# A graph attention layer before a mixture of experts: the opening rewritten up to the branch

## The chip, the cores and the metric

The program runs on one core of one Trainium2 chip. A core has TensorE (PE in the profile, its weight loads PEld), VectorE (DVE), ScalarE (ACT), GpSimd (POOL) and SyncE (SP), which issues transfers only. The metric is the device time of one execution in microseconds.

## The reference, cut to what matters

Everything is float32, with 4096 tokens of 256 numbers. The first part is a graph attention layer with four heads of 64, the second a mixture of 8 experts of which each token uses two. Only the first part is touched.

```python
xn  = layernorm(x)
h   = einsum('nd,hdk->hnk', xn, W)
s_col, s_row = (h * a1).sum(-1), (h * a2).sum(-1)
e   = leaky_relu(s_row[:, :, None] + s_col[:, None, :], 0.2)
att = softmax(where(adj > 0, e, NEG_INF), axis=-1)      # adj: 4096 x 4096
out = concat_over_heads(att @ h)
y   = elu(out) + xn @ Wr + br
x   = x + gamma * layernorm(y) + beta
x   = x + moe(layernorm(x))
```

## The kernel before, in words

The tokens are taken in 8 blocks of 512 (`B`), a block in four tiles of 128 (`TB`); two blocks make a range of 1024 rows (`R`, `HB` = 2), so there are four ranges. A softmax weight of a column token j and a row token i is made without an exponential of its own: up to a factor of the row that cancels, it is the larger of a row factor `er` and a column factor `eb`, masked by the adjacency; another column factor `ed` is multiplied into the projected values `ha`. VectorE does that in one instruction for a head and a tile j (`weigh`, L1353, `w<-er,eb,am`). TensorE multiplies `w` with `ha` into `acc` (L835) and with `unit` into `den` (L844), which sums the weights. `w` has ten buffers. This form holds only where the scores keep within a limit. A flag is computed from the weights; a branch goes to a general arm (not run with these inputs) or to the arm described here.

The row factors must stand along the free dimension and be the same on all 128 partitions, while the projection leaves them with a token on each partition. So `store_parts` transposes them to 16 rows, copies them (L792) and stores them to memory, and `load_rows` (L800) reads them back as a broadcast over all partitions.

**The opening, before the branch.** Small vectors and weights are loaded on ACT's queue, `x` by SP. 37 warm-up matmuls run (`WARM`). `norm_block(0)` computes mean and variance of block 0 (`bn_stats`, L176 and L177), one over the root by integer halving and three Newton steps (L159 to L168), scales the rows on ACT (L623), transposes them on TensorE (L630) and copies them out (L643). `scores_weights` multiplies W by a1 and a2, which gives eight more columns of the projection, and finds limit and flag. `project_first` projects block 0 into four accumulators (L747) and makes its factors, `factor_first` the scaled `ha`, `residual_first` xn @ Wr (L778). Then block 1 is normalised and transposed. Masks of the first tiles are made on ACT from adjacency slabs of 128x1024 (L1236).

**Behind the branch.** For the first four tiles j only the first half of range 0 is attended (block 0 is known), then the same tiles' second half, then full tiles. TensorE's order is written out by hand (`queue`, `order_of`, with `strict`): it follows the order of the program. `prepare_at(s)` stands between the tiles' matmuls and puts the preparation of the next block there, a piece for each step s: s = 0 to 3 follow the first halves, s = 4 to 7 the second halves, larger s the full tiles. `norm_steps` (statistics; ACT scaling; transposes) takes three steps and `project_steps` four. VectorE's and ACT's orders are made by the scheduler from priorities and dependencies; `tc.issue_after` holds a group of instructions behind a given one. Both arms are followed by the experts' stage, from some 785 us on.

## Time and profile before

| what | us |
|---|---|
| median of 3 runs (lowest, highest) | 1281.69 (1279.56, 1282.52) |
| the profiled execution | 1287.53 |
| its span, first to last instruction | 1285.8 |
| TensorE busy | 1255.5 |
| VectorE busy | 847.7 |
| the opening, to ACT's last work before the branch | 25.03 |
| TensorE's first attention matmul | 30.84 |
| TensorE's first full tile | 74.70 |
| TensorE's last attention matmul ends, about | 785.3 |

The profile shows one execution. A busy TensorE counts matmuls that overlap. "Granted clock" is the share of full speed that TensorE was given; its mean over the run is 0.996. In a timeline row the columns are start, duration, engine, line, operation, output and inputs; brackets hold the idle time before it and what ended it.

### The profile page before, as it was taken

The numbers are of one execution on the slowest core, as the hardware profiler recorded it, in microseconds if no ns is written. First come the engines' busy times: TensorE is split into PE (matmuls) and PEld (weight loads), VectorE is DVE, ScalarE is ACT, GpSimd is POOL, SyncE is SP. The second block draws the span as 40 slices with busy tenths as digits, with TensorE's granted clock in tenths as the row PEclk, the third lists the DMA queues.
The fourth block names the chain that finished last, engine by engine and source line by source line (L and its number), as shares of the span: only waits on it lengthen the run. The fifth ranks groups of instructions, "written<-read, shape, count | busy, mean of one in ns | idle before, by whom it ended". The sixth has DMA issues, their size and how long they took to land.

```text
span 1285.8 us, 23209 instructions
## 1 busy us (share of the span) xinstructions
PE 1255.5 (98%) x9073; PEld 685.4 (53%) x9073; DVE 847.7 (66%) x1623; ACT 463.3 (36%) x974; POOL 239.2 (19%) x196
## 2 busy tenths in 40 slices
PE   6999999999999999999999999998999999999997
PEld 4434444332232332332322325887888877888886
DVE  5799887879999999999999994934111121111110
ACT  4313222155522365421654313532333333233232
POOL 1000000001002701007010042245222212221212
PEclk9999999999999999999999999999999999999999
DMA  6523533336533746335463325978776776787782
GB/s 204 182 84 115 190 107 115 106 134 134 187 110 105 230 112 201 101 99 164 140 176 118 101 71 196 331 200 251 218 189 162 197 183 143 199 209 194 192 210 42
DMA packets 145010, 205.84 MB, mean 160 GB/s; under 512 B 49808, under 2 KB 113952, under 8 KB 144240
## 3 DMA queue, kind: packets, MB, share of 16 engines
q1 hardware_dynamic: 122432, 161.26, 40.8%
q0 software_dynamic: 20224, 35.68, 12.4%
q10 hardware_dynamic: 2224, 7.22, 1.6%
q8 instruction: 76, 1.25, 0.4%
q14 instruction: 54, 0.44, 0.1%
HBM read 171.89 MB, written 29.08 MB: 156 GB/s over the span
## 4 chain that ended last, share of the span: by engine, by line
PE 70%; DVE 6%; DMA 1%; issue 1%; SPq 1%; ACT 0%; POOLq 0%; DVEq 0%; ACTq 0%
PE acc L835 23%; PE po L1550 17%; PE ph L1519 17%; PE den L844 11%; DVE w L1353 4%; DMA early<-lists 1%; PE ptx L890 1%; PE pt L494 1%; PE ptr L1122 0%; PE pl L901 0%; DMA out<-o_last,ids 0%; SPq L1135 0%; SPq L1136 0%; POOLq L1681 0%; PE pd L1038 0%
## 5 line engine op out<-in xcount | busy, mean ns | idle before, releaser
L835 PE MATMUL acc<-w,ha 128*32 128x512 f32 x4096 | 670.4, 594 | 0.9 <-ACT u L1032 0.9
L1353 DVE SCALAR_TENSOR_TENSOR w<-er,eb,am 128x1024 f32<-128x1024 f32 x496 | 604.5, 1276 | 29.4 <-PE den L844 21.9
L844 PE MATMUL den<-w,unit 128*2 128x512 f32 x2048 | 465.5, 594 | 10.7 <-DVE w L1353 9.1
L835 PEld LDWEIGHTS acc<-w,ha 128*32 128x32 f32 x4096 | 182.2, 110 | 297.9 <-issue 265.2
L1236 ACT ACTIVATE am<-adj 128x1024 bf16<-128x1024 int32 x124 | 130.8, 1055 | 362.1 <-DVE w L1353 218.9
L1519 PE MATMUL ph<-xT,w 128*128 128x256 f32 (+1 forms) x1056 | 241.3, 386 | 4.3 <-DVE xT L498 3.1
L1550 PE MATMUL po<-w,hT 128*128 128x256 f32 x1088 | 240.2, 379 | 0.0
L1523 ACT ACTIVATE hT<-ph,bias 128x256 f32<-128x256 f32 (+1 forms) x264 | 126.2, 480 | 294.5 <-PE ph L1519 207.1
L1519 PEld LDWEIGHTS ph<-xT,w 128*128 128x128 f32 x1056 | 200.0, 190 | 40.2 <-DVE xT L498 3.5
L1550 PEld LDWEIGHTS po<-w,hT 128*128 128x128 f32 x1088 | 205.5, 190 | 27.7
L1561 DVE SCALAR_TENSOR_TENSOR o<-po,share,b2s 128x256 f32<-128x256 f32 x66 | 31.8, 482 | 261.0 <-PE po L1550 242.8
L844 PEld LDWEIGHTS den<-w,unit 128*2 128x2 f32 x2048 | 93.5, 85 | 163.0 <-issue 157.2
L1572 POOL DMA_INDIRECT out<-o,ids x66 | 103.0, 1561 | 334.1 <-DVE o L1561 157.3
L1016 POOL DMA_INDIRECT lists<-xe,at x64 | 93.6, 1463 | 267.0 <-issue 182.3
L498 DVE COPY xT<-pt 128x256 f32<-128x256 f32 x12 | 5.1, 424 | 61.3 <-PE pt L494 61.3
L725 POOL DMA_DIRECT2D residual<-rb x7 | 5.5, 779 | 159.2 <-DVE rb L720 136.6
L1542 ACT ACTIVATE b2s<-b2b,share 128x256 f32<-128x256 f32 x68 | 30.8, 503 | 0.0
L695 PE MATMUL ph<-wall,xT 128*128 128x264 f32 x112 | 28.8, 400 | 0.7 <-ACT xT L643 0.7
L695 PEld LDWEIGHTS ph<-wall,xT 128*128 128x128 f32 x112 | 20.0, 189 | 15.1 <-issue 8.7
L1072 POOL DMA_DIRECT2D xf<-in_x x6 | 8.1, 1345 | 100.3 <-ACT xf L1071 54.8
L702 PE MATMUL pr<-wr,xT 128*128 128x256 f32 x112 | 26.5, 379 | 0.0
L1353 DVE SCALAR_TENSOR_TENSOR w<-er,eb,er 128x512 f32<-128x512 f32 x32 | 22.3, 744 | 5.6 <-issue 5.6
(348 smaller groups left out, 632.7 us busy)
## 6 DMA issues: line engine op xcount, KB each, us to landing
w<-in_L_ffn_W SPq DMA_DIRECT2D x66, 1024.0 KB
adj<-in_adj SPq DMA_DIRECT2D x126, 512.0 KB
er<-parts ACTq DMA_DIRECT2D x3, 2048.0 KB
b2b<-in_L_ffn_b SPq DMA_DIRECT2D x33, 128.0 KB
early<-lists SPq DMA_DIRECT2D x16, 260.0 KB
residual<-rb POOLq DMA_DIRECT2D x8, 512.0 KB
rb<-residual SPq DMA_DIRECT2D x8, 512.0 KB
out<-y POOLq DMA_DIRECT2D x8, 512.0 KB
```

The costliest lines, as they stand in the source:

```text
L695: order_of(nc.tensor.matmul(phs[t - t0], xT[:, c, ts(t, P)], wall[:, c, :], start=(c == 0), stop=(c == DC - 1),))
L835: queue(nc.tensor.matmul(acc[half][h // 2][here : here + Q, :], ha[:, j, h * K + g * Q : h * K + (g + 1) * Q], w[half][h], start=(j == 0), ...
L844: queue(nc.tensor.matmul(den[here : here + HB, :], unit[:, j, h, 1 - half : 1 - half + HB], w[half][h], start=(j == 0 and half == 0), stop ...
L1016: ins = nc.gpsimd.indirect_dma_start(lists, bass.IndirectOffsetOnAxis(ap=at[:, k, t : t + 1], axis=0), xe[:, t, :], None,).ins
L1236: nc.scalar.activation(am, at, AF.Relu, scale=2.0)
L1353: nc.vector.scalar_tensor_tensor(wh[:, these], er[:, these, h], eb[:, j, h : h + 1], mask[:, these], op0=OP.max, op1=OP.min,)
L1519: order_of(nc.tensor.matmul(ph, job["w1"][:, c, ts(f, P)], xT[:, c, :], start=(c == 0), stop=(c == DC - 1),))
L1523: job["gelu"] = nc.scalar.activation(hT[:, f, :], ph, AF.Gelu, bias=job["bias"][:, f : f + 1]).ins
L1542: nc.scalar.activation(b2s[k], b2b, AF.Identity, scale=share[:, k : k + 1])
L1550: order_of(nc.tensor.matmul(po, hT[:, f, ts(k, CH)], w2[:, f, :], start=(f == 0), stop=(f == FC - 1)))
L1561: given_out.append(nc.vector.scalar_tensor_tensor(o, po, share[:, k : k + 1], b2s[k], op0=OP.mult, op1=OP.add).ins)
L1572: add()
```

## The change

- The weights of the scores are made by TensorE: `weights_turned` transposes W, and `scores_weights` multiplies it by `heads`, which POOL fills from a1 and a2 (two small loads instead of two broadcasts). The limit takes no Newton step, and its factor is 1.09 instead of 1.01.
- Block 0's rows are only centred (mean minus row) on ACT, tile by tile as statistics come; the transposed centred rows are projected, and one over the root (with its sign) is multiplied into scores and values behind the projection. The sum of the normalised rows comes from eight matmuls by the roots.
- `spread_parts` transposes a column of row factors broadcast over 128 columns, so that the result stands on all partitions, and ACT copies it to `er`. It replaces store and load for blocks 0 and 1.
- The opening's order is fixed on each engine as the program has it. There are 12 warm-up matmuls, then pairs.
- Block 1's norm and transposes and both blocks' residuals move behind the branch, into steps 0 to 3. Block 2's steps move from s = 1 to 7 on to s = 5 to 11, as the later blocks have them.
- In `measured`, used for blocks 1 to 7, the Newton steps run on POOL.
- The branch is a `Switch` with two arms; each engine reads the flag in the middle of the opening and is given a hint for the switch there.
- The loads of Wr and br move from ACT's queue to POOL's. The first slab is loaded ahead of block 1's rows.

```diff
-        ab = large("ab").rearrange("p t d -> p (t d)")[:, : 2 * HK]
-        ab = ab.rearrange("p (s k) -> p s k", s=2)
-        nc.scalar.dma_start(ab[:, 0], over_partitions(a1, HK))
-        nc.scalar.dma_start(ab[:, 1], over_partitions(a2, HK))
...
-        nc.scalar.dma_start(wr, Wr.rearrange("(c p) d -> p c d", p=P))
-        nc.scalar.dma_start(brm, over_partitions(br, D))
+        columns = gat.tile([P, 2, 2], F32)
+        for side, vec in enumerate((a1, a2)):
+            nc.scalar.dma_start(
+                columns[:, :, side],
+                bass.AP(tensor=vec.tensor, offset=vec.offset, ap=[[1, P], [P, 2]]),
+            )
...
+        nc.gpsimd.memset(heads, 0.0)
+        for i in range(2):
+            for q in range(2):
+                nc.gpsimd.tensor_copy(
+                    heads[ts(q, K), i, :, 2 * i + q], columns[ts(q, K), i, :]
+                )
...
+            nc.gpsimd.dma_start(wr, Wr.rearrange("(c p) d -> p c d", p=P))
+            nc.gpsimd.dma_start(brm, over_partitions(br, D))
...
+        def weights_turned():
+
+            pt = bank([P, 2, DC, P], "ptw")
+            for i in range(2):
+                for c in range(DC):
+                    order_of(nc.tensor.transpose(pt[:, i, c], wall[:, c, ts(i, P)], ident))
+            wT = large("wT").rearrange("p t d -> p (t d)")[:, : 2 * DC * P]
+            wT = wT.rearrange("p (i c d) -> p i c d", i=2, c=DC)
+            nc.scalar.copy(wT, pt)
+            return wT
+
+        def scores_weights(wT):
+
+            pw = bank([P, DC, 2 * H], "pw")
             for c in range(DC):
...
+                for i in range(2):
+                    order_of(nc.tensor.matmul(
+                        pw[:, c], wT[:, i, c], heads[:, i].rearrange("p s h -> p (s h)"),
+                        start=(i == 0), stop=(i == 1),
+                    ))
+            nc.vector.tensor_copy(wall[:, :, HK:], pw)
...
+            v, r = (gat.tile([P, H], F32, name=name) for name in ("vlim", "rlim"))
+            yield from root_steps(pl, v, r, H, 1.09 * D, steps=0)
+            nc.vector.scalar_tensor_tensor(limits[:, :H], v, -1.0, r, op0=OP.mult, op1=OP.mult)
+            yield
             nc.vector.tensor_tensor(limit, v, r, OP.mult)
-            nc.vector.tensor_scalar(limits[:, :H], limit, -1.0, None, op0=OP.mult)
+            yield
             wide = gat.tile([P, 1], F32)
             nc.vector.tensor_reduce(wide, limit, AX.X, OP.max)
-            marks["flag"] = nc.vector.tensor_scalar(
-                flag, wide, 0.5 * SPREAD, None, op0=OP.is_gt
-            ).ins
+            yield
+            nc.vector.tensor_scalar(flag, wide, 0.5 * SPREAD, None, op0=OP.is_le)
...
-            r, _ = root_of(mv[:, :, 1], TB)
...
+            v, r, off = sums_of("v"), sums_of("r"), sums_of("off")
+            beginning = root_steps(mv[:, :, 1], v, r, TB)
+            for _ in range(2):
+                next(beginning)
+            q = sums_of("q")
+            for _ in range(3):
+                nc.gpsimd.tensor_tensor(q, r, r, OP.mult)
+                nc.gpsimd.tensor_tensor(q, q, v, OP.mult)
+                nc.gpsimd.tensor_scalar(q, q, -0.5, 1.5, op0=OP.mult, op1=OP.add)
+                nc.gpsimd.tensor_tensor(r, r, q, OP.mult)
+            nc.gpsimd.tensor_tensor(q, mv[:, :, 0], r, OP.mult)
+            nc.gpsimd.tensor_scalar(off, q, -1.0, None, op0=OP.mult)
...
-        def norm_block(b, found=None):
-
-            found = found or measured(b)
+        def turn_block(b, xb):
+
             pt = banks_turned()
             for t in range(TB):
+                turn_row(pt, xb, t)
+            keep_turned(b, pt)
+
+        def norm_block(b, found=None):
+
+            found = found or measured(b)
+            for t in range(TB):
                 normal_row(found, t)
...
+            turn_block(b, found[0])
...
+        def in_trace_order(start):
+
+            before = {}
+            for ins in nc.cur_bb.bb.instructions[start:]:
+                if ins.engine in before:
+                    tc.add_manual_dep(
+                        ins, before[ins.engine],
...
+                    )
+                before[ins.engine] = ins.name
...
+        def open_first_block():
+
+            nc.scalar.activation(warm, tiny, AF.Exp)
+            xb = rows_loaded(0)
+            adj = load_adj(gat, range(R), 0, 1, 3)
+            second = rows_loaded(1)
+            other = load_adj(gat, range(R), 1, 1, 3)
...
+            rest_of_loads()
+
+            warm_up(12)
+            wT = weights_turned()
+            warm_up(2)
...
+            for t in range(TB):
+                st = small.tile([P, 6], F32, tag="st", name="st")
+                nc.vector.bn_stats(st, xb[:, t, :])
+                nc.vector.bn_aggr(mv[:, t, :], st)
+                nc.scalar.activation(
+                    xb[:, t, :], xb[:, t, :], AF.Identity, bias=mv[:, t, 0:1], scale=-1.0
+                )
+            for pair in range(TB // 2):
+                pt = bank([P, DC, 2, P], "pt")
+                for k in range(2):
+                    for c in range(DC):
+                        order_of(nc.tensor.transpose(
+                            pt[:, c, k], xb[:, 2 * pair + k, ts(c, P)], ident
+                        ))
+                    if pair + k == 0:
+                        scores_weights(wT)
+                    else:
+                        warm_up(2)
+                if pair == 0:
+                    sq = squares_of_weights()
+                (nc.scalar.copy, nc.vector.tensor_copy)[pair == 0](
+                    xT[:, :, ts(pair, 2 * P)], pt.rearrange("p c k i -> p c (k i)")
+                )
+            v, r = (gat.tile([P, TB], F32, name=name) for name in ("vrow", "rrow"))
+            limit_steps = limits_found(sq)
+            for _ in root_steps(mv[:, :, 1], v, r, TB, sign=-1):
+                next(limit_steps, None)
+            project_tile(0)
+            project_tile(1)
+            mask_of(adj[:, 0], first_masks[:, 0])
...
+            def scores(t):
+                nc.vector.scalar_tensor_tensor(
+                    sc[:, t], projected(t)[:, HK:], r[:, t : t + 1], limits,
+                    op0=OP.mult, op1=OP.add,
+                )
...
+                two = slice(t, t + 2)
+                nc.scalar.activation(unit[:, two, :, 1], cols[:, two], AF.Exp, scale=SLOPE)
+                nc.scalar.activation(eb[:, two, :], cols[:, two], AF.Exp, scale=1.0 - SLOPE)
...
+            def scaled(t):
+                nc.vector.scalar_tensor_tensor(
+                    ha[:, t, :].rearrange("p (h k) -> p h k", h=H),
+                    projected(t)[:, :HK].rearrange("p (h k) -> p h k", h=H),
+                    r[:, t : t + 1], unit[:, t, :, 1].unsqueeze(2).to_broadcast([P, H, K]),
+                    op0=OP.mult, op1=OP.mult,
+                )
+
+            for t in range(2):
+                scores(t)
+            factors(0)
+            project_tile(2)
+            mask_of(other[:, 0], first_masks[:, 1])
+            separate = nc.values_load(
+                flag[0:1, 0:1], min_val=0, max_val=1,
+                skip_runtime_bounds_check_because="a comparison gives 0 or 1",
+            )
...
+            tc.switch_hint(
+                {
+                    e: separate
+                    for e in (engines.PE, engines.DVE, engines.Activation, engines.Pool, engines.SP)
+                },
+                2, "way",
...
+            project_tile(3)
+            po = sums_of_first(xb, r)
+            for t in range(2):
+                scaled(t)
+            for t in range(2, TB):
+                scores(t)
+            nc.vector.tensor_scalar(
+                part.rearrange("p h t -> p t h"), rows, 0.0, None, op0=OP.max
+            )
+            nc.scalar.activation(part, part, AF.Exp, scale=SLOPE - 1.0)
+            factors(2)
+            for t in range(2, TB):
+                scaled(t)
+            nc.vector.tensor_copy(sums[:, :, 0], po)
+            spread_parts(part, er0[:, 0])
+            return r, second, separate
+
+        def sums_of_first(xb, r):
+
+            po = bank([P, DC], "po")
...
+                    order_of(nc.tensor.matmul(
+                        po[:, c : c + 1], xb[:, t, ts(c, P)], r[:, t : t + 1],
+                        start=(t == 0), stop=(t == TB - 1),
+                    ))
+            return po
...
+        def residual_pair(b, rb, t0):
...
+            if b in grown:
+                for k in range(2):
+                    nc.vector.scalar_tensor_tensor(
+                        rb[:, t0 + k, :], pr[:, k, :], grown[b][:, t0 + k : t0 + k + 1], brm,
+                        op0=OP.mult, op1=OP.add,
+                    )
+            else:
+                nc.vector.tensor_tensor(
...
+        def residual_steps(b):
...
+        def numbers_made():
...
+        def project_steps(b, apart, both=True):
...
+                if both:
+                    residual_pair(b, rb, t0)
...
+                marks["top"] = nc.vector.tensor_scalar(turn, rows, 0.0, None, op0=OP.max).ins
+                nc.scalar.activation(part, part, AF.Exp, scale=SLOPE - 1.0)
...
-            store_parts(b, part, nc.scalar if b == 1 else nc.gpsimd)
...
-        def factor_first():
...
-        def residual_first():
...
+            if both:
+                store_parts(b, part, nc.gpsimd)
+            else:
+                marks["eb"] = spread_parts(part, er0[:, 1])
...
+        def project_tile(t):
...
+        def spread_parts(part, er):
+
+            for h in range(H):
+                pe = bank([P, B], "pe")
+                for t in range(TB):
+                    order_of(nc.tensor.transpose(
+                        pe[:, ts(t, P)], part[:, h, t : t + 1].to_broadcast([P, P]), ident
+                    ))
+                ins = nc.scalar.copy(er[:, h], pe).ins
+            return ins
...
-        nc.scalar.activation(warm, tiny, AF.Exp)
-        marks = {}
-        norm_block(0)
-        second = rows_loaded(1)
...
-            scores_weights()
-        project_first()
...
-            second = measured(1, second)
...
-            factor_first()
...
-            residual_first()
-            norm_block(1, second)
-        load_rows(er0[:, :1], 0, 1, nc.sync)
...
+        opened = len(nc.cur_bb.bb.instructions)
+        r, second, separate = open_first_block()
+        in_trace_order(opened)
...
-        with tc.If(general > 0) as chosen:
+        ways = tc.Switch(separate, 2, hint="way")
+        if next(ways) == 0:
...
-        with chosen.Else():
+        if next(ways) == 1:
...
 
-                    for b in range(1, NB):
-                        first = {1: 0, 2: TB}.get(b, TB * b)
-                        if b > 1 and first - 3 <= s < first:
+                    if s == 0:
+                        with tc.issue_after(marks["w"]):
+                            numbers_made()
+                            found = measured(1, second)
+                        for t in range(TB):
+                            normal_row(found, t)
+                        for _ in residual_steps(0):
+                            pass
+                    if s == 1:
+                        turn_block(1, second)
+                        steps_of[1] = project_steps(1, True, False)
+                        next(steps_of[1])
+                    if s == 2:
+                        next(steps_of[1])
+                        next(steps_of[1])
+                    if s == 3:
+                        next(steps_of[1], None)
+                        for _ in residual_steps(1):
+                            pass
+                    for b in range(2, NB):
+                        first = TB * b
+                        if first - 3 <= s < first:
                             if b not in norms:
                                 norms[b] = norm_steps(b)
                             next(norms[b], None)
-                        if first <= s < first + (3 if b == 1 else 4):
+                        if first <= s < first + 4:
                             if s == first:
                                 steps_of[b] = project_steps(b, True)
                             next(steps_of[b], None)
-                            if b == 1 and s == first + 1:
-                                next(steps_of[b])
 
...
-                    if j == 2:
-                        load_rows(er[:, 1:], 1, 1, nc.sync)
```

## The prediction, made before the changed kernel was run

> **What bounds the kernel now.** I read the page's busy shares first, then the groups, then the opening in time order, because the change touches only the first 75 us of a span of 1285.8 us.
>
> ```profile
> PE 1255.5 (98%) x9073; PEld 685.4 (53%) x9073; DVE 847.7 (66%) x1623; ACT 463.3 (36%) x974; POOL 239.2 (19%) x196
> L835 PE MATMUL acc<-w,ha 128*32 128x512 f32 x4096 | 670.4, 594 | 0.9 <-ACT u L1032 0.9
> L1353 DVE SCALAR_TENSOR_TENSOR w<-er,eb,am 128x1024 f32<-128x1024 f32 x496 | 604.5, 1276 | 29.4 <-PE den L844 21.9
> L844 PE MATMUL den<-w,unit 128*2 128x512 f32 x2048 | 465.5, 594 | 10.7 <-DVE w L1353 9.1
> ```
>
> TensorE is the bound: VectorE's weights wait 21.9 us for TensorE to free them, while TensorE waits 9.1 us for VectorE in the whole run. All 9.1 lie in the opening. So whatever brings the first attention matmul forward moves the whole attention phase, and whatever is added to TensorE's queue behind the branch is paid in full. The timeline of the opening, around the branch (start, duration, engine):
>
> ```profile
> 19.82 0.34 SPq L793 DMA_DIRECT2D parts<-sp  x1
> 22.42 0.34 SPq L800 DMA_DIRECT2D er<-parts  x1
> 24.83 0.20 ACT L643 ACTIVATION_READ_ACCUMULATOR xT<-pt 128x1 f32 x1
> 29.02 2.00 ACT L1236 ACTIVATE er<-er 128x1024 bf16<-128x1024 int32 x2 [3.99 <-issue]
> 29.28 5.39 DVE L1353 SCALAR_TENSOR_TENSOR w<-er,eb,er 128x512 f32<-128x512 f32 x8 [5.59 <-issue]
> 30.84 1.02 PE L844 MATMUL den<-w,unit 128*2 128x512 f32 x2 [7.00 <-DVE w L1353]
> ```
>
> ACT's last work before the branch ends at 25.03; ACT, DVE and SP all resume between 29.0 and 29.3, so the branch costs 4.0 us. TensorE's first attention matmul is at 30.84. Stretches of one microsecond (PE busy, PEld, DVE, ACT, POOL, clock) show what the pause does:
>
> ```profile
> 27.00:28.00 1.00, 0.00 (x0) 0.00 (x0) 0.00 (x0) 0.00 (x0) 0.00 (x0) 1.00 0.80 258
> 28.00:29.00 1.00, 0.00 (x0) 0.00 (x0) 0.00 (x0) 0.00 (x0) 0.00 (x0) 0.73 0.26 90
> 34.00:35.00 1.00, 1.00 (x10) 0.52 (x6) 1.00 (x4) 0.00 (x0) 0.00 (x0) 0.50 0.80 207
> 35.00:36.00 1.00, 1.00 (x10) 0.01 (x2) 1.00 (x6) 0.00 (x0) 0.00 (x0) 0.86 0.96 340
> ```
>
> TensorE stops at 23.84; its clock halves at about 28.5, 4.6 us later, and comes back at about 35.3. Later there is one more hole, when the second block's row factors come back from memory:
>
> ```profile
> 58.08 6.04 DVE L1353 SCALAR_TENSOR_TENSOR w<-er,eb,er 128x512 f32<-128x512 f32 x9
> 59.54 1.03 PE L844 MATMUL den<-w,unit 128*2 128x512 f32 x4 [2.11 <-DVE w L1353]
> ```
>
> The first full tile (both halves) starts on TensorE at 74.70; from 59.54 on TensorE is busy without a break until 200.
>
> **Part 1, up to the branch.** Removed from this stretch: the second block's norm (stats, 12 root steps, ACT scaling 2.07, transposes 1.04, two ACT copies, together 20.33 to 25.03), the first residual (3.6 us of PE), and the trip of the row factors through memory (store 19.82, load 22.42). Block 0 now runs so:
> - Rows land as before; the last statistics row ends at 8.40. ACT centres each tile as it comes (0.52 to 0.60 each), the last to 9.0. The transposes of the second pair (0.13 each, from 8 in 1.04) end at 9.6, an ACT copy of 128x512 (0.60) at 10.2.
> - DVE copies the first pair (128x512 from PSUM, 0.68 by the residual row) to 9.4, then 11 root steps at 0.197 pitch: 11.6. The limit's steps are interleaved and fill the gaps of that pitch. PE projects four tiles meanwhile, 16 matmuls in 3.83: 10.0 to 13.9. No normalise pass stands between statistics and projection any more.
> - The scores take the root as a factor: 0.16 each from 11.7. The column sums are 16 instructions with one column; by the row of the limits (4 in 0.50) that is 2.0, so PE is free for the spreading at 15.9.
> - ACT has two masks (1.06 each) in between. The second waits for its adjacency slab; the same slab released its mask at 16.32 before. The first slab now stands before block 1's rows in SP's queue, and 256 KB of broadcast vectors are gone, so I take 15.0, and the mask ends at 16.1. Exponentials (0.2 each) follow to 16.7.
> - Spreading: 16 transposes (2.1 us) and four ACT copies of 128x512 (0.60 each, started at 17.0): 19.4.
>
> Sum: the branch is reached at 19.4 instead of 25.03, **-5.6**. Ends: 17.5 if the slab is early, 22.5 if it comes as late as 16.3 and the waits chain. The loads moved to POOL's queue (wr, brm) are not needed before the branch; the pair of tiny vector loads and POOL's five small steps hide behind the rows' 5.4 us of arrival, and cost up to 1 us if they come after the first transposes. Fewer warm-up matmuls cost nothing while the clock row stays at 1.00; at half clock the projections would add 3.8.
>
> **Part 2, the branch.** Nothing in the trace shows a hinted switch. Bounds: 0.1, what TensorE's exit from the present branch takes at 785.3, and 4.0, the entry now. What made the 4.0 is partly visible: each engine reads the flag between 22.7 and 24.5, while the broadcast of `er` fills the DMA engines to 26.4, and the fetches of code come only behind it:
>
> ```profile
> q8 instruction: 1, 0.02, 26.6%
> q14 instruction: 4, 0.03, 16.6%
> ```
>
> These are the code queues between 26.5 and 27.0. In the changed kernel neither the broadcast nor the residual's store is in flight then. I take 1.0: **-3.0**. The Trainium skill, "Runtime: NRT & Kernel Launch", Instruction fetch mechanics, says that a taken branch out of the window loaded in sequence must fetch its target first; it names no hint, so by it the 4.0 would stay and the total below would be 3.0 smaller. The new arm also ends in a jump, where the present one runs on; between nothing and 4.0 again. At the exit the chain runs through SP's loads (785.7 to 804.8) and TensorE idles 2.7 us of the next 35 anyway, so I cost it at nothing, with up to 2 without that cover.
>
> Then two weights (1.56, unchanged) give the first matmul at 22.0 instead of 30.84: **-8.8**. TensorE's pause would be about 3.5 us, below the 4.6 after which the clock fell.
>
> **Part 3, TensorE's queue behind the branch, to the same work done.** Added: the first residual (16 in 3.65), block 1's transposes with the wait for the ACT copies (1.04 + 0.7, as block 2 shows at 51.77 to 53.53), the spreading less the one transpose it replaces (2.1 - 0.3). Gone: the hole at 59.54 (2.1), block 2's wait of 0.7, since its projection now comes a tile later, and the half clock (5.2 us for the first half tile instead of 2.6). Block 2's projection moves four tiles on and costs the same there. 3.65 + 1.74 + 1.8 - 2.1 - 0.7 - 2.6 = **+1.8**; with a cold clock +4.4.
>
> **Part 4, a new wait.** TensorE's order is fixed: after the second half tile come block 1's transposes. TensorE gets there at 22.0 + 2.6 + 3.65 + 2.6 = 30.9. DVE starts at 20.4: four weights 2.7, the constants 0.65, statistics 2.6, two steps 0.4, to 26.8. Then 14 small POOL steps, for which the trace has no row of the kind: 0.13 (an iota of 128x8) to 0.28 (the select on 128x128) each, 1.8 to 3.9; I take 0.2, as DVE's pitch: 29.6. ACT's four scalings end at 31.7. Wait 0.8; if the next weights are interleaved with the statistics (4 x 0.67) it is 3.5. I take **+1.0**, range 0 to 5. The Trainium skill speaks against the move: "GPSIMD Engine Reference", 3.1, gives a 1.96 times slower add at 2048 elements and says to keep elementwise work on VectorE. An estimate by that ratio, from DVE's 0.16, is 4.4 us for the 14 steps, which makes this wait 2.4. In later blocks a whole tile (5.15) lies between these steps, and DVE is freed of some ten, where it isn't the bound: nothing.
>
> **Sum.** -8.8 + 1.8 + 1.0 = -6.0 us. The profiled execution took 1287.53 (1285.8 and 1.7 around it), so it would take 1281.5; the median of the runs, 1281.69, lies 5.8 lower, and I take the difference from it: **1275.7 us**. Its own range, by the ends: branch at 17.5, 0.1 of cost and no wait put the first matmul at 19.2, -11.7 + 1.8 = -9.9; branch at 21.0, 2 us of cost and 2 of wait put it at 24.6, -6.3 + 1.8 + 2 = -2.5.
>
> **Rivals.**
> - The hint does nothing and the clock falls: first matmul at 25.0, -5.9 + 4.4 + 1.0 = -0.5, **1281.2**, no change. For it: the 4.0 in the trace. Against: the load that delayed the fetch is gone.
> - The opening is bound by its loads: the second slab, ACT and the spreading end at 22.5, DMA being 0.94 to 0.99 busy from 5 to 15: first matmul at 25.1, -5.8 + 1.8 + 1.0 = -3.0, **1278.7**.
> - Slower: block 1's chain over POOL ends late and TensorE stands before its transposes. It decides from a wait of 4.6, an end at 35.5: there the clock halves as well (2.6), and -6.0 + 3.6 + 2.6 is no gain. POOL steps of 0.7 each (9.8 instead of 2.8) make the wait 8, of which 1.0 is counted: -6.0 + 7 + 2.6 = +3.6, **1285.3**. Against: the chain has 8.8 us of TensorE work as cover.
>
> **How the numbers follow.** What a measurement of this kernel can tell from no change is 0.2%, 2.6 us. Forecast 0.60; loads 0.12, of which half clears 2.6 us; no effect of the hint 0.14; slower by the wait 0.14, of which a little stays within 2.6. Faster 0.60 + 0.08 = 0.68, same 0.18, slower 0.14. The range runs from -10 to +0.8, 1271.7 to 1282.5, leaving out the wait's case and the far end of the gain.
>
> **What would show it.** Right: first `w` on DVE at 20 to 21 instead of 29.28, no `er<-parts` for the first two blocks, no clock of 0.50 behind the branch, first full tile some 14 us earlier (8.2 of it block 2's projection moved on), everything after 200 us shifted evenly by 6. Wrong: ACT idle before the second mask past 16; a gap of 4 us at the switch; TensorE waiting on `xb` at block 1's transposes; a hole at the exit that the loads don't cover.

## The result and the profile after

The changed kernel takes 1309.62 us (median of 4 runs, 1308.22 to 1311.96) against 1281.53 us for the kernel before on the same chip: a ratio of 1.0223 (95% interval 1.0204 to 1.0242). It is 28 us slower, where 1275.7 us was predicted (1271.7 to 1282.5). The experiments ran on other chips, where the kernel before had medians from 1283.7 to 1287.9, so all runs are compared by their ratio to it.

The page of the changed kernel (busy times, then the costliest groups; the last number is the idle time before the group and what ended most of it):

```profile
PE 1265.8 (97%) x9108; PEld 693.2 (53%) x9108; DVE 837.1 (64%) x1550; ACT 466.4 (36%) x980; POOL 276.1 (21%) x301
...
L1019 PE MATMUL acc<-w,ha 128*32 128x512 f32 x4096 | 671.2, 595 | 5.6 <-DVE w L1512 4.7
L1512 DVE SCALAR_TENSOR_TENSOR w<-er,eb,am 128x1024 f32<-128x1024 f32 x496 | 604.4, 1278 | 17.2 <-PE den L1028 10.3
L1028 PE MATMUL den<-w,unit 128*2 128x512 f32 x2048 | 465.3, 594 | 5.0 <-DVE token L132 5.0
...
L668 ACT ACTIVATE xb<-xb,off,r 128x256 f32<-128x256 f32 x28 | 14.5, 590 | 48.1 <-POOL off L662 48.1
...
L657 POOL TENSOR_TENSOR q<-r 128x4 f32<-128x4 f32 x21 | 10.9, 519 | 94.4 <-DVE r L158 93.3
```

The waits that the page puts down to VectorE (4.7 and 5.0) are together 9.7 us, about as long as before (9.1), and the 5.0 are the pause at the branch. New are ScalarE's 48.1 us in front of the scaling of a block's rows, for POOL's `off`, and a POOL instruction on 128x4 elements that takes 519 ns on average. The opening and the branch in order of time:

```profile
12.10 0.88 POOL L533 COPY heads<-columns 64x2 f32<-64x2 f32 x4 [9.21 <-DMA columns<-in_L_gnn_a]
12.57 1.91 PE L569 MATMUL pw<-heads,wT 128*128 128x8 f32 x8 [4.18 <-POOL heads L533]
...
24.71 0.39 SPq L643 DMA_DIRECT2D xb<-in_x  x1
29.19 2.74 DVE L1512 SCALAR_TENSOR_TENSOR w<-er,eb,er 128x512 f32<-128x512 f32 x4 [4.05 <-issue]
32.45 1.02 PE L1028 MATMUL den<-w,unit 128*2 128x512 f32 x2 [5.04 <-DVE token L132]
32.87 1.06 ACT L1420 ACTIVATE er<-er 128x1024 bf16<-128x1024 int32 x1 [4.84 <-issue]
```

TensorE had the first transposed rows at 8.40 and stood until 12.57 for `heads`, which POOL could not fill before the two loads of a1 and a2 had landed, 8.0 us after their issue. Behind the branch SyncE resumes at 24.71, and VectorE at 29.19, TensorE at 32.45 and ScalarE at 32.87, these three 4.0 to 5.0 us after their own last work. The first attention matmul is 1.6 us later than before, not 8.8 earlier. Stretches of five microseconds (PE busy, PEld, DVE, ACT, POOL, granted clock, DMA share, GB/s) show what the clock did:

```profile
15.00:20.00 5.00, 5.00 (x19) 3.50 (x17) 1.67 (x12) 1.54 (x2) 2.29 (x5) 0.56 0.51 127
25.00:30.00 5.00, 2.17 (x14) 1.52 (x11) 0.95 (x4) 2.25 (x4) 0.00 (x0) 0.62 0.81 284
30.00:35.00 5.00, 2.55 (x14) 0.64 (x18) 5.00 (x16) 2.00 (x2) 0.00 (x0) 0.50 0.39 148
```

The clock is 0.56 while the rows are transposed, behind the wait for `heads`, and 0.62 and 0.50 around the branch; there it had fallen at about 26.2 already, 1.2 us before TensorE's last work ahead of the branch ended. Of the waits (total, times, longest), two lines matter, the first of the whole run, the second from 60 to 330 us:

```profile
PE ph L909 <- ACT xT L691: 12.0, 6, 3.1
ACT xb L668 <- POOL off L662: 41.3, 6, 7.9
```

ScalarE stands six times for POOL, 7.9 us at the longest, and TensorE then waits for the copies of `xT`, which come from ScalarE. VectorE stands as well, since the exponentials that it needs come behind the scaling on ScalarE:

```profile
124.08 2.08 ACT L668 ACTIVATE xb<-xb,off,r 128x256 f32<-128x256 f32 x4 [7.89 <-POOL off L662]
127.24 0.42 DVE L921 TENSOR_TENSOR ha<-ph,unit 128x256 f32<-128x256 f32 x1 [6.55 <-ACT unit L920]
```

Where the 28 us went is read from three landmarks: the first attention matmul, the transposes of `ud` that close the first range, and those that close the last one.

| run | ratio to before (interval) | first attention matmul | first range closed | last range closed | span |
|---|---|---|---|---|---|
| before | 1 | 30.84 | 272.03 | 792.82 | 1285.8 |
| changed | 1.0223 (1.0204 to 1.0242) | 32.45 | 292.07 | 819.49 | 1307.3 |
| e1 roots on VectorE | 1.0147 (1.0098 to 1.0195) | 30.56 | 275.88 | 805.14 | 1299.4 |
| e2 no hold | 1.0207 (1.0160 to 1.0254) | 32.89 | 294.96 | 824.58 | 1317.8 |
| e3 columns first | 1.0144 (1.0090 to 1.0199) | 24.79 | 284.84 | 812.09 | 1304.8 |
| e4 If | 1.0264 (1.0214 to 1.0314) | 32.56 | 292.20 | 825.01 | 1315.0 |
| e5 own rows | 1.0113 (1.0064 to 1.0162) | 31.22 | 284.78 | 805.15 | 1302.6 |
| e6 columns, own rows | 1.0072 (1.0044 to 1.0099) | 25.60 | 278.48 | 798.86 | 1292.2 |
| e7 and roots on VectorE | 1.0019 (0.9987 to 1.0050) | 26.57 | 271.69 | 792.06 | 1288.9 |
| e8 before, roots on POOL | 1.0077 (1.0051 to 1.0104) | 29.10 | 280.58 | 801.29 | 1297.2 |
| e9 = e7, loads held | 0.9988 (0.9969 to 1.0008) | 22.37 | 270.69 | 791.07 | 1288.9 |
| e10 = e9, rows ahead of W | 1.0007 (0.9990 to 1.0025) | 23.75 | 271.34 | 791.76 | 1293.0 |
| e11 = e9, residual between | 1.0015 (0.9996 to 1.0034) | 25.04 | 273.27 | 793.64 | 1284.1 |
| e12 both orders | 1.0004 (0.9985 to 1.0024) | 22.14 | 269.65 | 790.02 | 1281.0 |

In the changed kernel 20.0 us are lost in the first range, of which only 1.6 stand before its first matmul, and 6.6 more in the three later ranges (527.4 against 520.8 us), which the change does not touch. Up to the end of the last range TensorE stands still for 30.6 us against 15.2, and is busy 11.2 us longer. The experts' stage, from the last range to the end, takes 487.8 us against 493.0; among all runs it lies between 488 and 501, so single spans are worth less than the landmarks. The first attention matmul is no exact measure either: e9 and e11 have the same opening, but W landed so that TensorE went on at 6.09 in one and at 7.82 in the other, and the matmul stands at 22.37 and 25.04.

### The profile page after: what moved, and what is told of

Its sections match the earlier page's. It is cut to its first block, busy times and chain, and to the rows that moved or that the text cites. A ratio compares the mean times of both kernels' runs of the same rounds, so it can differ in the third digit from the quotient of the medians.

```text
span 1307.3 us, 23382 instructions
## 1 busy us (share of the span) xinstructions
PE 1265.8 (97%) x9108; PEld 693.2 (53%) x9108; DVE 837.1 (64%) x1550; ACT 466.4 (36%) x980; POOL 276.1 (21%) x301
## 5 line engine op out<-in xcount | busy, mean ns | idle before, releaser
L1512 DVE SCALAR_TENSOR_TENSOR w<-er,eb,am 128x1024 f32<-128x1024 f32 x496 | 604.4, 1278 | 17.2 <-PE den L1028 10.3
L909 PE MATMUL ph<-wall,xT 128*128 128x264 f32 x112 | 32.2, 435 | 12.1 <-ACT xT L691 12.0
L921 DVE TENSOR_TENSOR ha<-ph,unit 128x256 f32<-128x256 f32 x28 | 11.4, 421 | 33.1 <-ACT unit L920 32.8
L668 ACT ACTIVATE xb<-xb,off,r 128x256 f32<-128x256 f32 x28 | 14.5, 590 | 48.1 <-POOL off L662 48.1
L657 POOL TENSOR_TENSOR q<-r 128x4 f32<-128x4 f32 x21 | 10.9, 519 | 94.4 <-DVE r L158 93.3
```

What stands on the lines that cost most here:

```text
L909: order_of(nc.tensor.matmul(phs[t - t0], xT[:, c, ts(t, P)], wall[:, c, :], start=(c == 0), stop=(c == DC - 1),))
L1512: marks["w"] = nc.vector.scalar_tensor_tensor(wh[:, these], er[:, these, h], eb[:, j, h : h + 1], mask[:, these], op0=OP.max, op1=OP.min,).ins
```

## The experiments

### First set: POOL's steps, the hold, the columns, the form of the branch

**e1.** `measured` finds its roots on VectorE again:

```diff
-            for _ in range(3):
-                nc.gpsimd.tensor_tensor(q, r, r, OP.mult)
...
-            nc.gpsimd.tensor_scalar(off, q, -1.0, None, op0=OP.mult)
+            r, _ = root_of(mv[:, :, 1], TB)
+            nc.vector.scalar_tensor_tensor(off, mv[:, :, 0], -1.0, r, op0=OP.mult, op1=OP.mult)
```

> The changed kernel with one thing undone: the Newton steps of blocks 1 to 7 are on VectorE again (L657 to L662 of the changed kernel become the twelve steps of before). Theory POOL: the steps on GpSimd last 1.1 to 1.2 us beside VectorE's weights instead of 0.2, ACT stands before the scaling, and the exponentials and masks behind it keep VectorE and then TensorE waiting. Then TensorE's waits for xT before the projections (12.0 us) fall under 3, range 0 ends 12 to 17 us earlier than at 282.3, and the time is 1292 to 1298. Rival HOLD: the statistics are late because they are held behind an earlier block's row factors, whatever engine takes the roots: 1303 to 1310.

Ratio 1.0147: some 10 us gained, less than expected. The first range gains 16.2 us (14.3 of them behind its first matmul), TensorE is busy for all of 100 to 200 us again (93 in the changed kernel); the later ranges gain nothing (529.3). POOL's steps matter, and something else does.

**e2.** Without the hold of statistics behind the factors of the block before:

```diff
-            with tc.issue_after(marks["top"]):
-                found = measured(b, fetched.pop(b))
+            found = measured(b, fetched.pop(b))
```

> The changed kernel without the hold on the statistics of blocks 2 to 7 (norm_steps measures as soon as rows are there); roots still on GpSimd. Theory POOL: the chain is still stretched beside the weights and still stands in ACT's queue, so most of the waits stay: 1300 to 1309. Rival HOLD: with the statistics some tiles earlier the chain has cover again, TensorE's waits for xT fall under 3 us: 1292 to 1298.

Ratio 1.0207, the changed kernel's: the hold is not the cause.

**e3.** a1 and a2 are loaded ahead of W on ScalarE's queue (the two blocks of code change places).

> The changed kernel with the two loads of single numbers (a1 and a2 as columns, 4 bytes an element) issued ahead of the weights on ACT's queue instead of behind them. Theory QUEUE: the 8.0 us to landing are time behind other transfers; then heads are filled at 4 to 7 instead of 12.1, TensorE's wait of 4.2 before them goes, its clock stays at 1.00 in the opening, the first attention matmul comes 5 to 8 us earlier than at 32.4 and the time is 1301 to 1305. Rival GRAIN: 512 elements of 4 bytes take that long wherever they stand: heads at 9 or later, time 1306 to 1311.

Ratio 1.0144, some 10 us gained. On TensorE:

```profile
8.40 0.96 PE L569 MATMUL pw<-heads,wT 128*128 128x8 f32 x8
24.79 1.02 PE L1028 MATMUL den<-w,unit 128*2 128x512 f32 x2 [5.48 <-DVE w L1512]
```

The wait for `heads` is gone, the projection starts at 11.57 in place of 18.93, and the first attention matmul stands at 24.79, 6.05 us ahead of the kernel before. The gain lasts: the last range closes 7.4 us earlier than in the changed kernel. Yet the run is slower than the kernel before by 18 us: nearly all of the loss lies behind the first matmul.

**e4.** `tc.If` with an `Else` in place of the `Switch`, and no hints.

> The changed kernel with the two arms under an if and else, as before the change, and without the hint. In the changed kernel each engine still pauses 4.0 to 5.0 us at the switch (SP from 20.7 to 24.7, VectorE 4.05, ACT 4.84, TensorE 5.04). Theory NO EFFECT: the hint did not prepare the code, so the if costs the same: pauses of 4 to 5 us, time within 3 us of the changed kernel's 1309.6. Rival HINT: the pause would be longer without it, or the if makes all engines wait for the last one as the 29.0 to 29.3 of before looked: first attention matmul 2 us or more later than 32.4, time 1312 or more.

Ratio 1.0264, with an interval that overlaps the changed kernel's. TensorE's pause is 4.19 us (5.04), ScalarE's 4.73 (4.84), and the first range closes at 292.20 (292.07): in one profile each, the hinted switch enters no faster than the plain branch. The longer time of this run comes from its later ranges.

### Second set: one of two row buffers

The traces of the first set showed row loads one after the other. In the changed kernel the rows of blocks 3 to 7 are loaded at 69.22, 107.78, 140.18, 172.67 and 205.23; the first of these is right behind block 2's transposes (68.09 to 69.18). In a later range, the timeline of POOL and ScalarE:

```profile
490.79 1.38 POOL L1256 DMA_DIRECT2D xf<-in_x  x1 [25.32 <-ACT xf L1255]
514.11 1.05 ACT L1255 COPY xf<-bet 128x1024 f32<-128x1024 f32 x1 [4.80 <-DMA y<-xf]
515.46 1.28 POOL L1256 DMA_DIRECT2D xf<-in_x  x1 [0.34 <-ACT xf L1255]
```

The second half's `xf` is copied only when the first half's sum `y<-xf` is through, 25 us behind the first `xf`. The second load of `rb` waited for VectorE's reading of the first:

```profile
SPq L1232 <- DVE y L1245: 2.5, 1, 2.5
```

All these tiles share two buffers (tag `loaded`), and behave as if there were one. By the program the other is kept: block 1's rows, loaded before the branch, are read in both arms since the change, so their buffer is freed behind the branch only.

**e5.** Block 1's rows are put into `u`, which is idle until the first range ends:

```diff
+        shared_u = fin.tile([P, HB, H // 2, B], F32, tag="u", name="u", bufs=1)
...
-            second = rows_loaded(1)
+            second = shared_u[:, 0].rearrange("p h b -> p (h b)")
+            second = second.rearrange("p (t d) -> p t d", t=TB)
+            nc.sync.dma_start(second, rows_of(x, 1))
...
-            u = fin.tile([P, HB, H // 2, B], F32, tag="u", name="u", bufs=1)
+            u = shared_u
```

> The changed kernel, with block 1's rows loaded into the space of the tile u, which is idle until the end of the first range, in place of one of the two row buffers (tag loaded). In the changed kernel block 1's rows are read in both arms of the branch, and its row loads follow each other as if one buffer were left: the second load of rb for a range waits for VectorE's reading of the first, the load of block b+1 for the transposes of block b. Theory BUFFER: the pinned buffer costs the later ranges 6.7 us together (174.1, 174.1 and 179.2 us against 172.6, 173.5 and 174.7) and in the first range it makes statistics late, so that POOL's chain of roots has no lead; the run is 7 to 17 us faster than the changed kernel, ratio to the kernel before 1.009 to 1.017, loads of x early, later ranges back to 172.6, 173.5 and 174.7. Rival POOL: POOL's chain sets the waits of the first range whatever the loads do, and the longer later ranges come from VectorE's order: under 4 us gained, ratio 1.019 to 1.024.

Ratio 1.0113. The later ranges take 172.55, 171.72 and 176.10, together 520.4: the whole loss there is gone. The two `xf` are loaded 3.7 us apart again:

```profile
476.62 1.37 POOL L1260 DMA_DIRECT2D xf<-in_x  x1 [19.98 <-ACT xf L1259]
480.34 1.28 POOL L1260 DMA_DIRECT2D xf<-in_x  x1 [2.35 <-ACT xf L1259]
```

The first range gains 7.3 (6.1 of them behind its first matmul). Theory BUFFER holds for the later ranges; POOL's chain, however, does not hide, as the next runs show.

**e6.** Columns first and own rows together.

> Both edits: a1 and a2 as columns loaded ahead of W on ScalarE's queue, and block 1's rows in the space of u. Theory BUFFER: the gains add, 7.7 us (the first attention matmul stood at 24.79 in place of 32.45 with the columns first) and 7 to 17 us: ratio 1.003 to 1.010. Rival POOL: only the columns count, ratio 1.012 to 1.018.

Ratio 1.0072: they add (first range 6.3 us shorter than e5, all but 0.7 of it before the first matmul).

**e7.** And the roots on VectorE.

> As the run before, and the Newton steps on VectorE again. Theory BUFFER: with a free buffer POOL's chain has a lead of a whole block and hides, so VectorE adds nothing: within 3 us of the run before, ratio 1.002 to 1.010. Rival POOL: the steps on VectorE are worth 9 us here as without the other edits, ratio 1.004 to 1.011 with the run before at 1.012 to 1.018. If both count fully: 1.0223 less 28 to 34 us, ratio 0.996 to 1.001.

Ratio 1.0019 and a first range 6.8 us shorter than e6: theory BUFFER, which said that POOL's chain would hide once rows come early, fell here; both count. From the changed kernel on, own rows, columns and roots take 7.3, 6.3 and 6.8 us off the first range (20.4, of 20.0 lost) and 14.3, 6.3 and 6.8 off the end of the last range (27.4, of 26.7). With these three the loss is gone.

The shares depend on the order in which the three are undone. From the first matmul to the end of the first range the kernel before takes 241.2 us, the changed kernel 259.6, e5 253.6, e1 245.3 and e7 245.1. So with the roots on VectorE the pinned buffer costs nothing in the first range (e1 against e7); with the roots on POOL it costs 6. And POOL's roots cost 14.3 there with the buffer pinned (changed against e1), but 7.8 with it free (e6 against e7). Only the loss in the later ranges is the buffer's whatever the roots do (7.0 us from the changed kernel to e5, 8.9 from e1 to e7).

**e8.** The kernel before with one part of the change alone, blocks 2 to 7 with their Newton steps and `off` on POOL.

> The kernel before, with one part of the change alone: the Newton steps and off of blocks 2 to 7 on POOL, 14 instructions a block. Its two row buffers are free and statistics run more than a block ahead of the scaling. Theory BUFFER: nothing to measure, ratio 0.998 to 1.003, since a longer chain is hidden by the lead. Rival POOL: the chain of 7 to 12 us beside VectorE's weights costs what it did in the changed kernel, 8 to 12 us, ratio 1.006 to 1.010.

Ratio 1.0077, 8.55 us in the first range (10.3 from its first matmul on, which came 1.7 earlier here) and none in the later ones (520.7): rival POOL holds. ScalarE's waits for `off` from 30 to 300 us, here and in the kernel before, and TensorE's here:

```profile
ACT xb L637 <- POOL off L625: 39.6, 6, 8.9
ACT xb L623 <- DVE off L615: 1.9, 1, 1.9
PE ph L709 <- ACT xT L657: 8.0, 3, 4.3
```

The lead of a block that was expected for the statistics is not there, in neither kernel: from the first step on the variance (`v`) to the scaling it is 2.6 to 11.0 us. What runs ahead is the scaling: in the kernel before block 5's stands at 124.68, and the copies of its `xT` at 156.41. So in both, on ScalarE, the scaling of block b + 1 stands ahead of the copies of `xT` and the exponentials of block b, and ScalarE's rows keep that order (in the changed kernel, whose rows are loaded later, ahead of the exponentials only). A longer chain to `off` makes TensorE wait for another block's copies. The longest of these waits, in e8, and the same place in the kernel before:

```profile
52.54 0.22 POOL L625 TENSOR_SCALAR off<-q 128x4 f32<-128x4 f32 x1
52.79 2.07 ACT L637 ACTIVATE xb<-xb,off,r 128x256 f32<-128x256 f32 x4 [5.03 <-POOL off L625]
55.49 3.89 PE L709 MATMUL ph<-wall,xT 128*128 128x264 f32 x8 [4.29 <-ACT xT L657]
...
50.34 0.60 ACT L623 ACTIVATE xb<-xb,off,r 128x256 f32<-128x256 f32 x1 [0.44 <-ACT sp L792]
53.53 2.18 PE L695 MATMUL ph<-wall,xT 128*128 128x264 f32 x8 [0.67 <-ACT xT L643]
```

Here all 14 steps of POOL's chain ran at 0.19 to 0.22 us, one each 0.28: 3.9 us where VectorE needs 1.9 for its ten in the kernel before. Beside VectorE's weights steps are longer still, as in the changed kernel:

```profile
118.31 1.16 POOL L657 TENSOR_TENSOR q<-r 128x4 f32<-128x4 f32 x1 [9.99 <-DVE r L158]
119.55 1.12 POOL L658 TENSOR_TENSOR q<-q,v 128x4 f32<-128x4 f32 x1
120.76 0.19 POOL L659 TENSOR_SCALAR q<-q 128x4 f32<-128x4 f32 x1
121.03 0.20 POOL L660 TENSOR_TENSOR r<-r,q 128x4 f32<-128x4 f32 x1
```

The first two stand beside two 1024-wide weights (VectorE, from 118.14 for 2.47 us); then VectorE waits for ScalarE, and the steps take 0.19 to 0.20. In each chain of the changed kernel two to six of the 14 steps are stretched, and a chain takes 5.4 to 8.6 us. How much of POOL's cost is the stretch, and how much the 14 steps at 0.28, no run separates.

### Third set: what is left at the branch and behind it

In e7 TensorE, ScalarE and VectorE end their work before the branch 3.3, 3.8 and 4.7 us earlier than in the kernel before, and it is no faster. Around its branch (first resumption of SyncE, VectorE, ScalarE, TensorE):

```profile
17.92 1.00 SPq L645 DMA_DIRECT2D xb<-in_x  x2
23.25 2.74 DVE L1509 SCALAR_TENSOR_TENSOR w<-er,eb,er 128x512 f32<-128x512 f32 x4 [4.26 <-issue]
26.30 2.00 ACT L1417 ACTIVATE er<-er 128x1024 bf16<-128x1024 int32 x2 [5.10 <-issue]
26.57 1.02 PE L1025 MATMUL den<-w,unit 128*2 128x512 f32 x2 [6.04 <-DVE token L132]
```

SyncE starts two row loads and three slabs at once; TensorE's pause is 6.04 us, ScalarE's 5.10.

**e9.** These loads are made to wait for the first weights:

```diff
-                fetched[2] = rows_loaded(2)
...
+                        with tc.issue_after(marks["first"]):
+                            fetched[2] = rows_loaded(2)
+                        tc.add_manual_dep(
+                            nc.cur_bb.bb.instructions[-1], marks["first"].name,
+                            mybir.DependencyInfo(
+                                mybir.DependencyClass.Sync, mybir.DependencyReason.DATA
+                            ),
+                            reason="loads behind the first weights",
+                        )
```

(and the same for the first slab).

> The run e7 (columns first, own rows, roots on VectorE), with the first loads behind the branch (rows of blocks 2 and 3, the first slabs) made to wait for VectorE's first weights. In e7 SyncE is through the branch at 17.92 and its loads fill the queues (391 GB/s from 20 to 25 us) while TensorE, idle from 20.52, waits for the packets that bring its code; its first attention matmul stands at 26.57 though the first weights are made at 24. Theory FETCH: the code stands behind the data, and TensorE's pause falls from 6.0 to 3.4 to 4.5 us, the first matmul at 24.0 to 25.1, 1.5 to 2.6 us gained, ratio 0.999 to 1.002. Rival ENTRY: the pause is the entry itself (3.4 to 6.0 us in the runs so far, whatever the loads do): first matmul at 26 to 27, ratio as e7, 1.001 to 1.004.

```profile
21.68 1.45 SPq L645 DMA_DIRECT2D xb<-in_x  x2
20.90 2.74 DVE L1518 SCALAR_TENSOR_TENSOR w<-er,eb,er 128x512 f32<-128x512 f32 x4 [3.26 <-issue]
22.23 2.00 ACT L1426 ACTIVATE er<-er 128x1024 bf16<-128x1024 int32 x2 [2.37 <-issue]
22.37 1.02 PE L1025 MATMUL den<-w,unit 128*2 128x512 f32 x2 [3.19 <-DVE w L1518]
```

The pauses fall to 2.37 us on ScalarE, 3.26 on VectorE and at most 3.19 on TensorE, which now waits for the weights; the first matmul comes 4.2 us earlier, 1.3 of them because W landed earlier in the opening. Theory FETCH holds for the pause. The DMA rows agree: in the changed kernel, e1 to e4, e6 and e7 the first attention matmul stands 2.4 to 2.7 us after a packet of 16 KB on code queue q8 begins, which I take for TensorE's code; it begins at 24.03 in e7, and at 17.63 in e9, before TensorE's work ahead of the branch is done. But the first range closes only 1.0 us earlier. TensorE waits for block 1's chain (0.51 us before the transposes, 0.67 for the copies) as in e7, but its clock is 0.50 to 0.54 from 22 to 28 and 0.52 to 0.63 from 38 to 42, where e7 had 1.00 from 30 on. From the first matmul to the end of the first range e9 to e12 take 247.5 to 248.3 us, e7 245.1. Ratio 0.9988, not told apart from the kernel before.

**e10.** In the opening the rows are centred and transposed ahead of W's transposes, and the roots come ahead of the copy of the products.

> As e9, with another order in the opening: ScalarE centres the four tiles as their statistics come and TensorE transposes them before the transposes of W (in the changed kernel ScalarE's copy of wT, which waits for W, stood ahead of the centring, at 8.30 in e7, and so the transposes of rows that had landed by 5.5 us began at 9.34); VectorE does the roots before it copies the products. Expected: the projection starts 2 to 2.6 us earlier (10.2 to 10.8 in place of 12.78), all that follows moves with it, and the time is 2 to 2.5 us below e9: ratio 0.996 to 1.000, faster than the kernel before by up to 0.4%. Rival: W arrives later still, or the clock falls in the pauses; then it is as e9.

Ratio 1.0007, a miss. The transposes started at 5.49 in place of 8.01, but the projection at 11.51 (11.44 in e9): TensorE reached W's transposes only at 8.10, behind the warm-ups that follow each tile. Then the clock was 0.66 from 10 to 15, and the projection took 5.43 us in place of 3.81.

**e11.** The second pair of block 0's residual moves behind block 1's transposes.

> As e9, with the second pair of block 0's residual moved behind the transposes of block 1, where TensorE waited 0.67 us for the copies of xT and then ran at clock 0.52 to 0.63 (38 to 42 us), and with two small instructions of numbers_made moved to step 2, so that block 1's factors are found earlier. Expected: block 1's projection starts at 37.5 to 38.5 at full clock in place of 37.62 to 41.13 at half, the second one at 42 to 43 in place of 43.99, 1 to 2 us gained on e9, ratio 0.996 to 0.999. Rival: TensorE now waits ahead of the transposes instead (ScalarE's scaling starts at 34.4), falls cold there, and nothing is gained: 0.998 to 1.000.

Ratio 1.0015: the rival held. TensorE now waits 3.19 us ahead of the transposes, and the way from the first matmul to the end of the first range is as in e9 (248.2 and 248.3 us).

**e12.** Both orders, with fewer warm-ups between the tiles.

> As e11, with the opening of e10 (rows centred and transposed ahead of W), but one warm-up in place of two after each tile and three behind the products, since e10's gain was lost to a clock of 0.66 from 10 to 15 us. Expected: the projection at 9.5 to 10.5 and at full clock (3.8 us), the first attention matmul at 20.5 to 22 in place of 22.37, up to 2 us below e11, ratio 0.994 to 0.998. Rival: the clock falls again in the shorter pauses, and it is as e11 or 1 us slower.

```profile
22.14 0.60 PE L1025 MATMUL den<-w,unit 128*2 128x512 f32 x2 [2.86 <-DVE w L1518]
34.07 2.17 PE L670 MATMUL pt<-ident,u 128*128 128x128 f32 x8 [4.14 <-ACT u L663]
```

The projection kept its clock (3.81 us) but began no earlier (11.54), and the clock was 1.00 through the branch. What was gained stands as a wait of 4.14 us for block 1's scaling. Ratio 1.0004. So no run was shown to beat the kernel before: the three faults can be taken out of the change, and what is left of it, even with the loads held, is worth nothing that these runs could measure.

## Why the prediction was wrong, point by point

- **Where the sum went**: it said -8.8 us up to the first attention matmul, +2.8 from there through the first range and nothing later; measured are +1.6, +18.4 and +6.6.
- **What bounds the kernel**: right. TensorE stayed the bound, and what was lost were its gaps (15.4 us more up to the end of the last range) and its clock (busy 11.2 us longer).
- **Part 1, up to the branch at 19.4**: right but for one term. With the columns first, ScalarE's last copy ends at 19.98 (e3). The failed term is "the pair of tiny vector loads ... hide behind the rows' 5.4 us of arrival, and cost up to 1 us". They landed 8.0 us after their issue behind W's loads, and with the halved clock that followed they cost 5.6 (e5 to e6) to 7.7 us (changed kernel to e3). The slab, to which I gave a rival, was never waited for.
- **Part 2, the branch at 1.0**: the size was wrong. The pauses were 4.0 to 5.0 per engine. I blamed the broadcast of `er` for the slow fetch of code, and had it gone; but SyncE, through the branch first, starts the next loads itself (e7 against e9). The Trainium skill, "Runtime: NRT & Kernel Launch", Instruction fetch mechanics, which I had set against my 1.0, says that a taken branch out of the window loaded in sequence must fetch its target first; the runs agree, with pauses of 2.2 to 6.2 us on TensorE and ScalarE and no run without one. The 4.6 us after which I took the clock to fall were no threshold: it fell 1.8 us after TensorE's last work in e9, 2.0 after in e11 and e7, and 1.2 before it in the changed kernel.
- **Part 3, +1.8, or +4.4 with a cold clock**: from the first matmul to the end of the first range e7, with its roots on VectorE, takes 245.1 us and the kernel before 241.2, so +3.9, where Parts 3 and 4 said +2.8, or +5.4 with a cold clock. The clock was cold (0.50 to about 29.4 in e7), a case that the sum left out.
- **Part 4, the new wait**: at block 1's transposes there was none, but by luck. POOL's 14 steps took 5.4 us (36.22 to 41.63) instead of 2.8, and the chain from VectorE's first weight to `off` 12.4 instead of 9.2; TensorE came to the transposes 11.0 us after its first attention matmul instead of 8.9, its clock being halved. With the clock at 1.00, the roots on VectorE and half of the residual moved away, it waited 4.14 (e12). The step that failed is "In later blocks a whole tile (5.15) lies between these steps ... nothing". POOL's 14 steps there cost 6.8 (e6 to e7) to 8.55 us (e8), and 14.3 together with the pinned buffer (e1). I had bounded a step by 0.13 and 0.28, from POOL rows of the opening, where VectorE makes no weights, and asked whether TensorE's next step had cover, not what is queued behind ScalarE's wait. The Trainium skill, "GPSIMD Engine Reference", 1. Specifications, says that GpSimd shares its SBUF interfaces with VectorE and names contention with VectorE instructions that have two SBUF inputs. The weights are such instructions, and the rows agree: 0.2 us alone, 1.1 beside them. I had drawn on 3.1 of that page alone, whose factor of 1.96 is the smaller one here.
- **Not in the prediction at all**: the pinned row buffer, 14.3 us to the end of the last range when it is freed first (e5), as much as the roots when these are moved first (e1). I had listed block 1's norm as moved behind the branch, without asking which tiles now live across it and what else takes turns in their buffers. "Everything after 200 us shifted evenly" was therefore wrong too: the later ranges grew by 6.6 us.
- **The rivals**: the slower one named POOL's chain, but at block 1 and with a total of +3.6 us; the place and the size were wrong. That the hint does nothing came true (4.0 to 5.0 us, and no shorter than the plain branch of e4), at a price beside which the rest counted more.

## What to carry to other kernels

When work moves across a branch, list the tiles that now live on both sides of it, and count the buffers that are left for everything that shares their tag; the loss shows up as loads that start one by one, far from the edit. A step given to a slower engine is priced beside what the other engines run at that time, and by what is queued behind the engine that waits for it. After a branch, the first engine through it can fill the queues that the others' code must come by.

## What the hardware did that was not expected

- POOL instructions of 128x4 elements stretched from 0.19 us to nearly the length of the weight beside them (in the changed kernel 0.53 to 0.75 with 512 columns, 1.10 to 1.26 with 1024). Beside VectorE's `rb<-pr,brm` (58.73 for 0.68 us), which reads one input from PSUM, they took 0.20.
- Two loads of 1 KB, four bytes a piece, took 8.0 us to land behind W's loads; ahead of them, POOL could read both 3.4 us after the first one's issue (e7).
- With the loads held (e9 to e12) TensorE's pause at the branch was 2.7 to 3.2 us and ScalarE's 2.2 to 2.6; with a hinted switch and loads not held 3.4 to 6.2 and 4.6 to 5.8. The one short pause of TensorE among these (e5, 3.35) had its 16 KB packet on q8 at 25.62, 0.9 us after the loads began and 2.2 before TensorE's last work ended.
- Pauses of nearly equal length left the clock differently: after 2.86 us (e12) the first attention matmul took 0.60 us, after 2.74 (e11) 1.02. In e11 the clock had halved 2.0 us after TensorE's last work, in e9 1.8, in the kernel before 4.6.
